# One layer-pair kernel for a graph and expert network on one core: gathered rows added by the DMA that gathers them, a multiplication moved to GpSimd, and other step lengths in the planner

## The chip, the cores and the metric

The kernel runs on one core of a Trainium2 chip. A core has five engines that each work through their own list of instructions in order: TensorE (PE; its weight loads are shown apart as PEld), VectorE (DVE), ScalarE (ACT), GpSimd (POOL) and SyncE (SP, which here only issues DMA transfers). Sixteen DMA engines move the data that any of them asks for. The metric is the device time of one launch in microseconds (us); lower is better.

## What is computed

Two layers over 2708 rows of 256 channels, in float32. Each layer has a graph attention over a 2708 x 2708 matrix and then a mixture of 8 experts of which every row uses 2; the first layer also has causal attention before its experts. Cut to what matters here:

```python
def _L0_gnn_ref(nodes, adj_bias_mat, weight, conv_weight1, conv_weight2, bias):
    h = nodes @ weight
    logits = h @ conv_weight1 + (h @ conv_weight2).T
    coefs = softmax(leaky_relu(logits, 0.2) + adj_bias_mat, axis=-1)
    return coefs @ h + bias

def _L0_ffn_ref(x, ...):                       # T = 2708, 4 heads, 2 key heads, head size 64
    h = _rmsnorm(x, ln1_w); q, k, v = h @ wq.T, h @ wk.T, h @ wv.T     # then rotary on q and k
    att = softmax(where(causal, q @ k.T / sqrt(64), -1e30))
    x = x + (att @ v) @ wo.T
    flat = _rmsnorm(x, ln2_w)
    # top 2 of 8 experts by softmax(flat @ router_w.T), weights normalised to sum 1
    out = sum(weights[:, e:e+1] * ((silu(flat @ w1[e].T) * (flat @ w3[e].T)) @ w2[e].T) for e in range(8))
    return x + out

x = x + _L0_gnn_ref(_layernorm(x), adj, ...)
x = x + _L0_ffn_ref(_layernorm(x)[None], ...)[0]
x = x + _L1_gnn_ref(_layernorm(x), adj, ...)   # masked by adj != 0 or the diagonal
x = x + _L1_ffn_ref(_layernorm(x)[None], ...)[0]
```

In the first layer the matrix holds values up to 1e9 that are added to the logits. So each row's softmax picks the one column with the largest value, and the graph attention of a row is the row of h at that column. The kernel uses this: it searches the largest value of each matrix row and its index, and gathers that row of h. (It counts whether the two largest values lie far enough apart, and would run a general version otherwise.)

## The kernel before

The rows are cut into 22 tiles of 128 (the last has 20). Four stages follow each other on the core: `first` (graph and causal attention of layer 0, its routing, and some blocks of its experts), `experts_blocks` for layer 0, `second` (graph attention of layer 1, its routing) and `experts_blocks` for layer 1. In the trace, the experts' first matmul (line 2015) of layer 0 begins at 526.7 us.

**The order of the work in `first` and `second`** comes from a planner, `Plan` (line 70). Each step is added with an engine, a planned length in us, the steps it needs, the buffers it takes and gives back, a rank, and for transfers a time `lands` until the data is there. `Plan.issue` then simulates the engines with these lengths and writes the instructions in the order in which the steps start, the lowest rank first among those that can start soon. Only the order comes from the lengths; on the chip each engine takes its list in this order and waits for semaphores where it must. Where the planner sees TensorE idle for 1 us or more, `fill` puts in matmuls that nobody uses (tile `nobody`, line 1259), to keep TensorE's clock up.

**What `first` does for each tile** (`tile_in`, line 956):

- `load`: SyncE loads 128 rows of the matrix (1354 KB) into one of three places of `arena`.
- `top` and `index` (lines 968 and 972): VectorE searches the largest values of each row and the index of the largest.
- `narrow` and `save`: ScalarE casts the matrix tile to bfloat16, SyncE stores it for layer 1.
- `fetch` (line 987): GpSimd issues an indirect DMA that gathers for each of the 128 rows the row of `hd` (h in DRAM, written by `project`) at the found index into a tile `xg`, 3 buffers.
- `stats` (line 995): VectorE adds `xg` to the tile of `X` (which lies in SBUF for the whole stage) and takes mean and variance of the sum. `power` and `norm`: GpSimd and ScalarE normalise it into `XB`.
- `turn`, `back`, `times`, `leave`: TensorE transposes the tile of `X`, multiplies it by the query, key and value weights, ScalarE moves the result.
- `both` (on GpSimd): the rotary step; `turn_qk` and `keep`: its transposition into `qT` and `kT`.

Before the tiles, `project` computes h for each pair of tiles; its step `bias` (line 904) adds the graph attention's bias to `X` on GpSimd. The list `biased` holds these steps; `stored` holds the writes of h.

**The causal attention** runs by pairs of tiles (`pair`, line 1074). For a pair that starts at tile t0: scores and their exponentials block by block, causal masks on GpSimd (`mask`, line 1104), the products with V on TensorE (`values`), and from the fourth pair on the sums of the exponentials on VectorE (`sums`, line 1131, tile `es`). Then:

- `leave`: ScalarE copies the products to `ob` in SBUF.
- `spread` (line 1167): TensorE brings the sums to all partitions, in a PSUM bank of the kind `mm` (2 banks).
- `weigh` (line 1176): VectorE takes the reciprocal of the sums into `yT` and multiplies `ob` by it. It gives back the `mm` bank and `ob`.
- `project_out`, `join`, `sum_up`, `store`: the output projection for each tile of the pair, its additions to `XB` and `X`, and the store.

GpSimd's list holds, besides the steps named, the scatters of routed rows to the experts' buffer (line 1803) and the accumulations of expert results in DRAM (`add_rows`, line 609). VectorE's list holds the searches, statistics, sums and routing, in one order.

In `second`, five loads bring `X` back from DRAM (line 1511); their steps have planned landing times.

Of the kernel before, what the change touches and what calls it, by code (L numbers as in the profile page):

```python
# [10 lines left out]
F32 = mybir.dt.float32  # L11
AF = mybir.ActivationFunctionType
ALU = mybir.AluOpType
AX = mybir.AxisListType
I32 = mybir.dt.int32
BF16 = mybir.dt.bfloat16
NEEDS = mybir.DependencyInfo(mybir.DependencyClass.Sync, mybir.DependencyReason.DATA)
PE, SP = mybir.EngineType.PE, mybir.EngineType.SP
PSUM = bass.MemoryType.PSUM

P = 128
N = 2708
C = 256
# [5 lines left out]
NREP = NH // NKV  # L29
# [14 lines left out]
LATE, LATE_T = ((7, 4), (7, 5)), 12  # L44
# [25 lines left out]
class Plan:  # L70
# [16 lines left out]
    def add(self, engine, length, run, needs=(), take=(), give=(), rank=0.0, lands=0.0):  # L87
        step = dict(engine=engine, length=length, run=run, needs=[n for n in needs if n is not None],
                    take=take, give=give, rank=rank, lands=lands, end=None)
        self.steps.append(step)  # L90
        return step
# [54 lines left out]
def adj_ffn_kernel(ctx, tc, x, adj, vecs, bias_rows, tab, w_gnn0, w_gnn1, wqkv, wo,  # L146
                   r0, r1, w1_0, w3_0, w2_0, w1_1, w3_1, w2_1, out):
    nc = tc.nc
# [633 lines left out]
    def first(X, XB, norms, tops, hd, mb, xs, acc, arena, load_weights):  # L782
# [11 lines left out]
        with ExitStack() as s:  # L794
            ap = s.enter_context(tc.tile_pool(name="attn", bufs=1))
            af = s.enter_context(tc.tile_pool(name="af", bufs=2))
            adjp = s.enter_context(tc.tile_pool(name="adjf", bufs=3))
            ab = s.enter_context(tc.tile_pool(name="ab", bufs=2))
# [20 lines left out]
            def tr_tile():  # L819
# [3 lines left out]
                        z=2, qk=2, es=1, ob=2, yT=2, mb=2, rT=1, adj0=1, adj1=1, adj2=1, low0=1, low1=1, low2=1)  # L823
            add = plan.add
# [3 lines left out]
            for a, b in ((0, 4), (4, NT - 1)):  # L828
                loads.append(add("SP", 0.5, lambda a=a, b=b: nc.sync.dma_start(
                    out=X[:, a:b, :], in_=x[a * P:b * P, :].rearrange("(t p) c -> p t c", p=P)),  # L830
                    rank=-9.0, lands=1.5 + 0.4 * (b - a)))
            loads.append(add("SP", 0.5, lambda: nc.sync.dma_start(
                out=X[:rows(NT - 1), NT - 1, :], in_=x[(NT - 1) * P:N, :]), rank=-9.0, lands=9.0))
# [20 lines left out]
            a = add("SP", 1.2, load_wq, loads, take=["e"], rank=1.5, lands=3.0)  # L854
# [22 lines left out]
            centred = centre(wgc, wg[0], C, [wg_in], -3.0), centre(wq_sb, wq_sb, 2 * C, [wq_in], -0.5)  # L877

            stored, biased = [], []
# [76 lines left out]
            def tile_in(t):  # L956
                r = rows(t)
                v = {}
                rank = float(t)
# [24 lines left out]
                def save(h):  # L984
                    nc.sync.dma_start(out=mb[t * P:(t + 1) * P, h * HALF:(h + 1) * HALF], in_=v["m", h])

                def fetch():
                    v["xg"] = af.tile([P, C], F32, tag="xg", name="xg", bufs=3)
                    nc.gpsimd.indirect_dma_start(
                        out=v["xg"][:r], out_offset=None, in_=hd[:, :],  # L990
                        in_offset=bass.IndirectOffsetOnAxis(ap=v["ix"][:r, 0:1].bitcast(I32), axis=0))

                xt = X[:r, t, :]

                def stats():
                    nc.vector.tensor_tensor(xt, xt, v["xg"][:r], ALU.add)
                    v["mv"] = moments(xt, r)
                    v["pv"] = small.tile([P, 2], F32, tag="pv2", name="pv2")
                    nc.vector.scalar_tensor_tensor(v["pv"][:r], two_eps[:r, 0, :], v["mv"][:r, 1:2], two_eps[:r, 1, :],
                                                   ALU.mult, ALU.add)  # L1000
# [45 lines left out]
                def keep():  # L1046
# [3 lines left out]
                a = loaded[t] = add("SP", 5.8, load, take=[f"adj{t % 3}", f"low{t % 3}", "tb"], rank=rank,  # L1050
                                    lands=1.5)
                a = add("DVE", 2.97, top, [a], rank=rank + 2)
                b = a
                for h in range(2):

                    b = add("ACT", 1.4, lambda h=h: narrow(h), [b, stored[-1]], take=["mb"], give=[f"low{t % 3}"] * h, rank=rank + 4)
                    add("SP", 0.4, lambda h=h: save(h), [b], give=["mb"], rank=rank, lands=3.0)
                a = add("DVE", 3.05, index, [a], take=["ix"], give=[f"adj{t % 3}"], rank=rank + 2)
                a = add("POOL", 1.1, fetch, [a] + stored, take=["xg"], give=["ix"], rank=rank, lands=2.2)
                a = add("DVE", 1.4, stats, [a, biased[t]], take=["mv"], give=["xg"], rank=rank)  # L1060
                c = add("POOL", 1.2, power, [a], give=["mv"], rank=rank)
                b = add("ACT", 0.6, norm, [c], rank=rank)
                a = add("PE", 0.5, turn, [a], take=["mm"], rank=rank)
                a = add("ACT", 0.4, back, [a], take=["hT"], give=["mm"], rank=rank)
                a = add("PE", 2.0, times, [a, centred[1]], take=["mm"], give=["hT"], rank=rank)
                c = add("ACT", 0.8, leave, [a, c], take=["z"], give=["mm"], rank=rank)
                a = add("POOL", 3.4, both, [c], take=["qk"], give=["tb"], rank=rank)
                add("ACT", 0.7, lengths, [c, a], give=["z"], rank=rank + 6)
                a = add("PE", 0.65, turn_qk, [a], take=["mm"], give=["qk"], rank=rank)
                a = add("ACT", 0.7, keep, [a], give=["mm"], rank=rank)  # L1070
                made[t] = a, b

# [1 line left out]
            def pair(t0):  # L1074
# [3 lines left out]
                v = {}  # L1078
                on_pe = t0 < PE_SUMS
                rank = t0 + 2.5  # L1080
                ready = [made[t0][0], made[t0 + 1][0]]
                end = None
# [4 lines left out]
                for n in range(0, t0 + 2, 2):  # L1087
# [54 lines left out]
                    es = []  # L1142
                    for sb in two:
                        a = add("PE", 1.0, lambda f=scores, sb=sb: f(sb), ready, take=["st"], rank=rank)
# [4 lines left out]
                        es.append(b)  # L1149
                    last = n == t0  # L1150
                    if on_pe:
                        end = add("PE", 3.0, values, es + [end], take=["o", "zs"] if n == 0 else [],
                                  give=["e"] * 2, rank=rank)
                        ends = [end]
                    else:
                        end = add("PE", 2.0, values, es + [end], take=["o"] if n == 0 else [], rank=rank)
                        ends = [add("DVE", 2.4 if n else 1.2, sums, es + [ends[0] if n else None, end],
                                    take=["es"] if n == 0 else [], give=["e"] * 2, rank=rank)]

                def leave():  # L1160
# [6 lines left out]
                def spread():  # L1167
# [3 lines left out]
                    else:  # L1171
                        for g in range(NKV):
                            nc.tensor.matmul(v["z"][g * HD:(g + 1) * HD, :], allones[:, :HD], v["es"][:, g, :],
                                             start=True, stop=True)

                def weigh():
                    v["yT"] = ab.tile([P, 2, NREP, P], F32, tag="yT", name="yT")
                    y = v["yT"].rearrange("p t j c -> p (t j c)")
                    nc.vector.reciprocal(y, v["z"])
                    nc.vector.tensor_tensor(y, v["ob"], y, ALU.mult)  # L1180

                a = add("ACT", 1.2 if on_pe else 0.6, leave, [end], take=["ob", "es"] if on_pe else ["ob"],
                        give=["o", "zs"] if on_pe else ["o"], rank=rank - 1)
                a = add("PE", 1.0, spread, [a] + ends, take=["mm"], give=["es"], rank=rank - 1)
                a = add("DVE", 4.2, weigh, [a], take=["yT"], give=["mm", "ob"], rank=rank - 1)
                for i in range(2):
                    t = t0 + i
                    r = rows(t)

                    def project_out(i=i, t=t, r=r):  # L1190
                        v["pw", i] = pw = mm_tile()
                        for j in range(NREP):
                            nc.tensor.matmul(pw[:r, :C], v["yT"][:, i, j, :r], wo_sb[:, j, :],
                                             start=(j == 0), stop=(j == NREP - 1))

                    def join(i=i, t=t, r=r):
                        nc.vector.tensor_tensor(XB[:r, t, :], v["pw", i][:r, :C], XB[:r, t, :], ALU.add)

                    def sum_up(t=t, r=r):
                        nc.gpsimd.tensor_tensor(out=X[:r, t, :], in0=X[:r, t, :], in1=XB[:r, t, :], op=ALU.add)  # L1200

                    def store(t=t, r=r):
                        nc.sync.dma_start(out=acc[t * P:t * P + r, :], in_=X[:r, t, :])

                    b = add("PE", 1.0, project_out, [a], take=["mm"], give=["yT"] if i else [], rank=rank - 1)
                    b = add("DVE", 0.45, join, [b, made[t][1]], give=["mm"], rank=rank - 1)
                    joined.append(b)
                    b = add("POOL", 1.1, sum_up, [b], rank=rank + 3)
                    summed.append(b)
                    add("SP", 0.4, store, [b], rank=rank + 3)  # L1210
# [197 lines left out]
    def second(X, XB, xs0, x1, x2, sd, mb, xs, arena, load_weights):  # L1408
# [9 lines left out]
        with ExitStack() as s:  # L1418
# [93 lines left out]
            for a, b in zip((0,) + ends, ends):  # L1512
                loads.append(add("SP", 0.45 * (b - a), lambda a=a, b=b: nc.sync.dma_start(
                    out=X[:, a:b, :], in_=x1[a * P:b * P, :].rearrange("(t p) c -> p t c", p=P)),
                    late, rank=-9.0, lands=2.0 if 0 < a < LATE_T else 7.0))
                if b == LATE_T:
                    late = some_blocks(add, 0, [(*b, []) for b in LATE], [XR[:, k, :] for k in range(len(LATE))], [],
                                       lambda e: weights_at(arena[:, WE:]), xs0, x1, new, named, -20.0)
                    for e in late:
                        e["needs"] += loads  # L1520
# [697 lines left out]
```

## Time and profile before

| what | us |
|---|---|
| median of 3 runs (lowest, highest) | 1566.0 (1564.26, 1569.35) |
| the profiled execution, its own time | 1573.58 |
| its span, from the first to the last instruction | 1571.9 |
| `first`, 0 to 527 us of the span: PE, DVE, ACT, POOL busy | 466.4, 397.8, 296.6, 270.6 |
| experts of layer 0, 527 to 867 us: PE busy | 339.8 of 340 |
| `second`, 867 to 1216 us: PE, DVE busy | 333.0, 209.0 of 349 |
| experts of layer 1, 1216 to 1572 us: PE busy | 340.4 of 356 |
| granted TensorE clock, mean | 0.969 |

All views below are of this one profiled execution. In a line of a group of instructions stand line, engine, operation, output and inputs with their shapes, the count, then the busy us in total and the mean in ns of one, then the idle time of the engine just before them and what ended it. In a line of the waits stand who waited, for whom, us in total, how often and, where it is given, the longest. In a line of a stretch stand its bounds and length, and per engine the busy us and the count of instructions. TensorE instructions are recorded twice for each float32 matmul, so counts of records are twice those of matmuls.

### The profile page before, as it was taken

The numbers are of one execution on the slowest core, as the hardware profiler recorded it, in microseconds if no ns is written. First come the engines' busy times: TensorE is split into PE (matmuls) and PEld (weight loads), VectorE is DVE, ScalarE is ACT, GpSimd is POOL, SyncE is SP. The second block draws the span as 40 slices with busy tenths as digits, with TensorE's granted clock in tenths as the row PEclk, the third lists the DMA queues.
The fourth block names the chain that finished last, engine by engine and source line by source line (L and its number), as shares of the span: only waits on it lengthen the run. The fifth ranks groups of instructions, "written<-read, shape, count | busy, mean of one in ns | idle before, by whom it ended". The sixth has DMA issues, their size and how long they took to land. (4 is left out here: it accounts for less than half of the span.)

```text
span 1571.9 us, 23225 instructions
## 1 busy us (share of the span) xinstructions
PE 1479.6 (94%) x8926; PEld 1154.0 (73%) x8926; DVE 747.2 (48%) x1483; ACT 552.5 (35%) x1068; POOL 500.9 (32%) x684
## 2 busy tenths in 40 slices
PE   6888899989999999999999799999999999999996
PEld 5633333323335999999999778888768999999995
DVE  5798899876576222222221464857754222222221
ACT  3676567555544111111221353443332111111110
POOL 5654468483152222222112210030434122222221
PEclk9989899999999999999999899999999999999998
DMA  7688654650012323333221670632414233332211
GB/s 261 225 286 298 209 194 176 198 171 7 8 49 80 88 53 88 90 91 89 35 38 22 152 150 1 131 89 82 146 53 112 78 83 87 74 76 62 33 33 17
DMA packets 165998, 165.68 MB, mean 105 GB/s; under 512 B 81378, under 2 KB 145550, under 8 KB 163168
## 3 DMA queue, kind: packets, MB, share of 16 engines
q1 hardware_dynamic: 142582, 134.26, 28.0%
q0 software_dynamic: 19024, 26.24, 9.2%
q10 hardware_dynamic: 4270, 3.58, 0.7%
q8 instruction: 72, 1.18, 0.3%
q14 instruction: 50, 0.41, 0.1%
HBM read 87.38 MB, written 61.55 MB: 95 GB/s over the span
## 5 line engine op out<-in xcount | busy, mean ns | idle before, releaser
L2015 PEld LDWEIGHTS pup<-xTs,arena 128*128 128x128 f32 x2772 | 317.8, 190 | 3.7 <-ACT xTs L283 0.7
L2015 PE MATMUL pup<-xTs,arena 128*128 128x128 f32 x2772 | 319.7, 275 | 0.5 <-ACT xTs L283 0.5
L2020 DVE TENSOR_TENSOR hT<-sl,pup 128x640 f32<-128x640 f32 x87 | 71.4, 821 | 448.0 <-ACT sl L2019 448.0
L2019 ACT ACTIVATE sl<-pup 128x640 f32<-128x640 f32 x87 | 61.3, 704 | 503.3 <-PE pup L2015 499.2
L1576 PE MATMUL po<-hb,PT 128*128 128x257 f32 (+2 forms) x968 | 226.0, 388 | 3.6 <-DVE PT L1569 3.6
L1576 PEld LDWEIGHTS po<-hb,PT 128*128 128x128 f32 (+2 forms) x968 | 176.1, 188 | 42.6 <-issue 11.9
L2029 PE MATMUL y<-arena,hT 128*128 128x256 f32 x756 | 173.8, 380 | 0.6 <-DVE ys L2031 0.6
L1101 ACT ACTIVATE e<-stt 128x1024 f32<-128x1024 f32 (+1 forms) x132 | 125.9, 985 | 93.6 <-PE stt L1095 69.2
L2029 PEld LDWEIGHTS y<-arena,hT 128*128 128x128 f32 x756 | 138.7, 190 | 17.3 <-DVE ys L2031 1.0
L1140 DVE TENSOR_TENSOR es<-es,e 128x1024 f32<-128x1024 f32 x104 | 130.6, 1256 | 31.2 <-ACT e L1101 24.5
L611 POOL DMA_INDIRECT out<-ys,xt x44 | 68.4, 1554 | 231.1 <-DVE ys L2031 221.9
L1095 PE MATMUL stt<-qT,kT 64*128 64x512 f32 (+1 forms) x528 | 133.4, 612 | 6.7 <-ACT e L1101 6.7
L1803 POOL DMA_INDIRECT xs<-XR,place x88 | 95.2, 1081 | 135.0 <-DVE mk L1563 40.7
L611 POOL DMA_INDIRECT acc<-ys,xt x43 | 66.9, 1555 | 222.6 <-DVE ys L2031 221.1
L1121 PE MATMUL o<-e,V 128*64 128x512 f32 (+1 forms) x528 | 129.7, 614 | 1.2 <-ACT e L1101 1.2
L2015 PE MATMUL pup<-xTs,room 128*128 128x128 f32 (+1 forms) x1056 | 123.8, 275 | 0.0
L2015 PEld LDWEIGHTS pup<-xTs,room 128*128 128x128 f32 (+1 forms) x1056 | 121.9, 190 | 1.2
L1554 ACT ACTIVATE E<-sb,dcol 128x768 f32<-128x768 f32 (+1 forms) x88 | 75.2, 859 | 105.0 <-DVE PT L1569 102.1
L1095 PEld LDWEIGHTS stt<-qT,kT 64*128 64x128 f32 x528 | 44.0, 187 | 80.2 <-issue 62.9
L1121 PEld LDWEIGHTS o<-e,V 128*64 128x64 f32 x528 | 34.1, 141 | 73.0 <-issue 54.3
L2031 DVE TENSOR_SCALAR ys<-y,xt 128x256 f32<-128x256 f32 x87 | 42.0, 483 | 53.9 <-PE y L2029 53.9
L2029 PE MATMUL y<-room,hT 128*128 128x256 f32 x288 | 66.1, 379 | 0.0
(276 smaller groups left out, 1885.6 us busy)
## 6 DMA issues: line engine op xcount, KB each, us to landing
arena<-in_adj SPq DMA_DIRECT2D x21, 1354.0 KB
arena<-in_w SPq DMA_DIRECT2D x36, 640.0 KB
mb<-mb SPq DMA_DIRECT2D x44, 352.0 KB
xs<-none SPq DMA_DIRECT2D x16, 804.0 KB
xt<-xs SPq DMA_DIRECT2D x87, 134.0 KB
room<-in_w SPq DMA_DIRECT2D x12, 640.0 KB
acc<-X SPq DMA_DIRECT2D x21, 128.0 KB
out<-X SPq DMA_DIRECT2D x21, 128.0 KB
```

The lines of the kernel that those rows point to most:

```text
L611: nc.gpsimd.indirect_dma_start(out=acc[:, :], out_offset=bass.IndirectOffsetOnAxis(ap=xt[:, C:C + 1].bitcast(I32), axis=0), in_=ys, in_off ...
L1095: nc.tensor.matmul(st[:r, g, c0(sb):], kT[a:b, sb * P:sb * P + r], qT[a:b, t0 + (sb == t0 + 1):t0 + 2, :, :], start=True, stop=True)
L1101: nc.scalar.activation(e[:r, :, c0(sb):], v[sb, "st"][:r, :, c0(sb):], AF.Exp, scale=1.0 / HD ** 0.5)
L1121: nc.tensor.matmul(v["o"][g * HD:(g + 1) * HD, c:], V[:r, sb, g * HD:(g + 1) * HD], v[sb][:r, g, c:], start=(n + i == 0), stop=(n + i == t ...
L1140: nc.vector.tensor_tensor(es, es, v[sb][:r, :, c:], ALU.add)
L1554: nc.scalar.activation(e[:q, :n], sb[:q, i0:i1], AF.Exp, bias=dcol[:q, j:j + 1], scale=SLOPE - 1.0)
L1576: nc.tensor.matmul(v["po", i][:r, :F], v["PT", j][:q, a:a + r], hb[:q, j, :], start=(j == 0), stop=(j == NT - 1))
L1803: i = nc.gpsimd.indirect_dma_start(out=xs[:, :], out_offset=bass.IndirectOffsetOnAxis(ap=at, axis=0), in_=src, in_offset=None)
L2015: nc.tensor.matmul(pp[:to, n, :], wn[:, c, :], xT[:, c, :], start=(c == 0), stop=(c == KC - 1))
L2019: nc.scalar.activation(sl, pp[:, :NF, :], AF.Silu)
L2020: nc.vector.tensor_tensor(hT[:, :NF, :], sl, pp[:, NF:2 * NF, :], ALU.mult)
L2029: nc.tensor.matmul(y, hT[:, n, :], w[3][:, n, :], start=(n == 0), stop=(n == NHC - 1))
```

## The change

Three edits, all in `first` but for one number in `second`:

1. `fetch` gathers straight into the tile of `X` and has the DMA add to what stands there (`compute_op=ALU.add`). The tile `xg` and the addition in `stats` go. `fetch` now needs the tile's `bias` step. (`xg` stays as the name of the buffers of some experts' results.)
2. `weigh` is cut in two: the reciprocal stays on VectorE (`turn_over`, gives back the `mm` bank), and the multiplication by it goes to GpSimd (`weigh`, gives back `ob`).
3. Planned lengths: several of TensorE's and VectorE's steps, and the landing time of the first load of `X` in `second`.

```diff
+                xt = X[:r, t, :]
+
                 def fetch():
-                    v["xg"] = af.tile([P, C], F32, tag="xg", name="xg", bufs=3)
                     nc.gpsimd.indirect_dma_start(
-                        out=v["xg"][:r], out_offset=None, in_=hd[:, :],
-                        in_offset=bass.IndirectOffsetOnAxis(ap=v["ix"][:r, 0:1].bitcast(I32), axis=0))
-
-                xt = X[:r, t, :]
+                        out=xt, out_offset=None, in_=hd[:, :],
+                        in_offset=bass.IndirectOffsetOnAxis(ap=v["ix"][:r, 0:1].bitcast(I32), axis=0),
+                        compute_op=ALU.add)
 
                 def stats():
-                    nc.vector.tensor_tensor(xt, xt, v["xg"][:r], ALU.add)
                     v["mv"] = moments(xt, r)
...
-                a = add("POOL", 1.1, fetch, [a] + stored, take=["xg"], give=["ix"], rank=rank, lands=2.2)
-                a = add("DVE", 1.4, stats, [a, biased[t]], take=["mv"], give=["xg"], rank=rank)
+                a = add("POOL", 1.6, fetch, [a, biased[t]] + stored, give=["ix"], rank=rank, lands=2.5)
+                a = add("DVE", 0.95, stats, [a], take=["mv"], rank=rank)
...
-                a = add("PE", 0.5, turn, [a], take=["mm"], rank=rank)
+                a = add("PE", 0.25, turn, [a], take=["mm"], rank=rank)
...
-                a = add("PE", 2.0, times, [a, centred[1]], take=["mm"], give=["hT"], rank=rank)
+                a = add("PE", 1.75, times, [a, centred[1]], take=["mm"], give=["hT"], rank=rank)
...
-                a = add("PE", 0.65, turn_qk, [a], take=["mm"], give=["qk"], rank=rank)
+                a = add("PE", 0.35, turn_qk, [a], take=["mm"], give=["qk"], rank=rank)
...
-                        end = add("PE", 3.0, values, es + [end], take=["o", "zs"] if n == 0 else [],
+                        end = add("PE", 2.9, values, es + [end], take=["o", "zs"] if n == 0 else [],
...
-                        end = add("PE", 2.0, values, es + [end], take=["o"] if n == 0 else [], rank=rank)
-                        ends = [add("DVE", 2.4 if n else 1.2, sums, es + [ends[0] if n else None, end],
+                        end = add("PE", 1.9, values, es + [end], take=["o"] if n == 0 else [], rank=rank)
+                        ends = [add("DVE", 2.46 if n else 1.25, sums, es + [ends[0] if n else None, end],
...
+                def turn_over():
+                    v["yT"] = ab.tile([P, 2, NREP, P], F32, tag="yT", name="yT")
+                    nc.vector.reciprocal(v["yT"].rearrange("p t j c -> p (t j c)"), v["z"])
+
                 def weigh():
-                    v["yT"] = ab.tile([P, 2, NREP, P], F32, tag="yT", name="yT")
                     y = v["yT"].rearrange("p t j c -> p (t j c)")
-                    nc.vector.reciprocal(y, v["z"])
-                    nc.vector.tensor_tensor(y, v["ob"], y, ALU.mult)
+                    nc.gpsimd.tensor_tensor(out=y, in0=v["ob"], in1=y, op=ALU.mult)
...
-                a = add("PE", 1.0, spread, [a] + ends, take=["mm"], give=["es"], rank=rank - 1)
-                a = add("DVE", 4.2, weigh, [a], take=["yT"], give=["mm", "ob"], rank=rank - 1)
+                a = add("PE", 0.9, spread, [a] + ends, take=["mm"], give=["es"], rank=rank - 1)
+                a = add("DVE", 3.4, turn_over, [a], take=["yT"], give=["mm"], rank=rank - 1)
+                a = add("POOL", 1.6, weigh, [a], give=["ob"], rank=rank - 1)
...
-                    b = add("PE", 1.0, project_out, [a], take=["mm"], give=["yT"] if i else [], rank=rank - 1)
+                    b = add("PE", 0.9, project_out, [a], take=["mm"], give=["yT"] if i else [], rank=rank - 1)
...
-                    late, rank=-9.0, lands=2.0 if 0 < a < LATE_T else 7.0))
+                    late, rank=-9.0, lands=2.0 if 0 < a < LATE_T else 14.0 if a == 0 else 7.0))
```

## The prediction

> **What bounds the kernel now.** I read the table of stages first: the change touches the first stage (0 to 527 us of the span), and in the third only one planned landing time. The chain of waits shows only the last 5 us here, so I took the busy times of all engines in the two halves of the first stage, then the slices of the page, then who waited for whom.
>
> ```profile
> core 0: us, PE busy (x) PEld busy (x) DVE busy (x) ACT busy (x) POOL busy (x), PEclk, DMA share, GB/s
> 60.00:340.00 280.00, 243.36 (x993) 100.84 (x993) 245.55 (x277) 183.59 (x323) 171.60 (x250) 0.92 0.65 223
> 340.00:527.00 187.00, 177.54 (x860) 82.51 (x861) 112.68 (x169) 89.26 (x148) 64.68 (x97) 0.98 0.18 58
> ```
>
> From 60 to 340 us VectorE is busy 245.6 of 280 us, and TensorE 243.4: TensorE idles 36.6 us there and only 9.5 us in the 187 us after it. The max and index searches over the adjacency rows (22 of each, 2.97 us a piece) end at 326.8 us; until then VectorE's in-order list sets the pace, after it TensorE does. The waits of the first stage (who waited for whom, us in total, times, longest) say what the idle time of both was:
>
> ```profile
> DVE X L996 <- DMA xg<-hd,ix: 19.8, 9, 3.6
> ...
> PE pm L1044 <- POOL qk L1038: 11.9, 9, 3.3
> PE stt L1095 <- ACT e L1101: 6.7, 6, 3.3
> PE pm L1173 <- DVE es L1140: 5.9, 3, 2.9
> PE pm L1193 <- DVE yT L1180: 4.6, 6, 1.1
> ```
>
> VectorE's largest wait is for the gathered rows (19.8 us). TensorE's waits are short and spread: each is for a step that follows VectorE's list.
>
> The pieces that the change moves:
>
> ```profile
> L996 DVE TENSOR_TENSOR X<-X,xg 128x256 f32<-128x256 f32 (+1 forms) x22 | 10.8, 490 | 19.9 <-DMA xg<-hd,ix 19.8
> L1180 DVE TENSOR_TENSOR yT<-osb,yT 128x512 f32<-128x512 f32 x11 | 8.6, 784 | 1.1
> L989 POOL DMA_INDIRECT xg<-hd,ix x22 | 24.9, 1131 | 29.0 <-DVE ix L972 20.4 <-issue 8.3 <-ACT mb L982 0.2
> L611 POOL DMA_INDIRECT acc<-ys,xt x43: 1550/1551/1569, 540.8 to 862.4; - x43
> ```
>
> **What the Trainium skill says.** "DMA: Bandwidth & Descriptors", section SWDGE vs HWDGE vs iDMA: an accumulating DMA can only be issued from GpSimd, and each DMA engine takes turns between its queues packet by packet. The trace has both kinds of transfer; the queue's line for one gather of 128 rows, and for one accumulation of 128 rows (7 us windows both):
>
> ```profile
> q0 software_dynamic: 48, 0.13, 6.3%
> ...
> q0 software_dynamic: 144, 0.13, 16.1%
> ```
>
> Same bytes, three times the packets, and 1.13 instead of 0.44 us of each DMA engine. The same page, section Rules for kernel authors: an accumulating DMA must wait for earlier writers of its bytes; so the gather must now follow the bias add of its tile of x. "SBUF — State Buffer", section Who interferes with whom: a VectorE instruction with two SBUF inputs and a GpSimd instruction that reads SBUF exclude each other. The trace agrees: the rotary add L1038 takes 0.99 us alone and 1.86 us at 320.9 us beside two sums L1140, which then take 3.38 instead of 2.5 us. "GPSIMD Engine Reference", section Performance versus the Vector engine: two-input arithmetic is about twice as slow there; here 128x256 takes 0.73 us and 128x384 1.00 us on GpSimd, so I estimate 1.27 us for 128x512, against 0.69 us on VectorE.
>
> **The change part by part** (the built order of both kernels is known, their times not).
>
> *Adds leave VectorE.* 22 adds by 0.490 us: -10.8 us, all before 340 us. TensorE's transposition of x can then start without the add, too.
>
> *Multiplications leave VectorE.* 11 by 0.784 = 8.6 us, of which 7 (5.5 us) start before 340 us, where VectorE counts. The four later ones are hidden behind TensorE already, and I cost them at nothing.
>
> *The gather becomes an accumulation.* On GpSimd's queue 1.55 instead of 1.13 us, 22 by 0.42 = +9.2 us; 11 multiplications add 14 us. GpSimd's busy time from 60 to 340 us goes from 172 to about 190 of 280 us: room, but everything there is in order. What counts is the landing. Where VectorE waited, the gathered rows had landed 6.4 to 8.6 us after the gather began on GpSimd under load (118.37 to 126.94, 77.36 to 84.70), and 2.5 us in the quiet (331.61 to 334.10). The new one takes +0.4 us to issue, +0.7 us of transfer, and, for six more turns of each engine beside the adjacency loads, an unknown rest. Bounds: below by nothing (a part may overlap); above by about 5 us, if each extra packet waits like a gather's own under load. Nearest evidence: the accumulation at 503.62, beside weight loads (DMA 0.9 busy), had all its packets done by about 508.6, 5 us after its start. I take +1.5 us in all.
>
> What that costs follows from the slack, the VectorE work that stands between an index search and the statistics that need its rows. Counting instructions of the built orders by their measured lengths, the slack before is under 8 us for 13 of 22 tiles. Stalls summed as (landing minus slack): 17 us at a landing of 7 us, 28 at 8; the measured 19.8 fits 7.3 us. After, fewer tiles are short (8 under 8 us): 15 us at 8, 25 at 9, 35 at 10, 49 at 11, 63 at 12. At 7.3 + 1.5 = 8.8 us: 23 us, +3 against before.
>
> *The multiplication waits on GpSimd.* It waits for the reciprocal; behind it in GpSimd's order stand mostly the causal masks (L1110 before), for which TensorE's products wait. And in 5 of 11 pairs VectorE's next instruction after the reciprocal is a sum of two SBUF tiles (1.22 us), which excludes the multiplication. Bounds 0 and 11 by 1.3 = 14 us; mostly GpSimd is the one that is held, so I take 1.5 us on VectorE in its critical part. The output projection gets its input about 0.8 us later than now; other TensorE work stands beside it, and without that cover it would be 11 by 0.8 = 9 us.
>
> *Lengths.* They change the order only. The planner now thinks TensorE shorter, sees more gaps and puts in 31 more idle matmuls in this stage (110 instead of 79). At 0.327 us each 10 us, if the gaps weren't there; TensorE does idle 36.6 us in the part where nearly all of them stand, so nothing is charged. By the order, the last index search comes after 252 instead of 282 us of VectorE work: tiles are prepared sooner, sums later. In the third stage the landing of the first x tiles (planned 7, now 14 us) swaps some statistics before 911 us, where the first product waited for the mask's DMA anyway: 0, within 2 us either way.
>
> *Sum.* VectorE's part to the last index: -10.8 - 5.5 + 3 + 1.5 = -11.8 us. TensorE must fill the time: its idle there would fall from 36.6 to 25 us, but part of it hangs on GpSimd's rotary work (11.9 us), which gets later. I pass on two thirds: -8 us. The profiled execution took 1573.58 us, span 1571.9, so 1565.6 for it; it lies 7.6 us above the median of the runs, 1566.0, from which I forecast **1558 us**.
>
> **The rivals.**
> *A, as above:* 1546 to 1561 us. For it: VectorE busy 88% where TensorE idles, and TensorE at 95% right after. Chance 0.55.
> *B, the relief is absorbed:* TensorE takes no more than now, since its own clock (granted 0.92 in this part), the masks and rotary work on the fuller GpSimd, and the additional idle matmuls hold it. Then the 11.8 us become VectorE idle: about 1565 us, 1561 to 1571. For it: 11.9 us of TensorE's waits are for GpSimd already; against: GpSimd has 90 us of room. Chance 0.24.
> *C, slower:* the accumulating gather lands too late, at the statistics of each tile, with the next max and index search in order behind them. It decides from a landing of about 10 us, 3 us later than the gather's: there the stalls, 36 us less the 20 of now, have eaten the 16.3 us of adds and multiplications that leave. At 12 us they are 63, 43 more than now, so VectorE's list is 27 us longer; half to two thirds of that reach the end: about 1582 us. At 11 us it is about 1573. For it: three times the packets in turn-taking with loads that keep the DMA engines 65% busy; against: the loaded accumulation at 503.62. Chance 0.21.
>
> **How the numbers follow.** About 0.3%, 4.7 us, is what this measurement can tell from no change. Faster (below 1561.3): A and a little of B, 0.57. Same: most of B and the mildest of C, 0.22. Slower (over 1570.7): 0.21. A's own range is 1546 to 1561. The range reaches up through B into C as far as a landing of 11 to 12 us, and down to all of VectorE's gain with fewer stalls: 1543 to 1577.
>
> **What would show it.** Right: no VectorE add after the gather; VectorE's last index search ends near 312 us instead of 326.8; its waits for the gathered x stay near 20 us; TensorE's idle from 60 to 340 us falls under 30 us; the experts' first matmul comes near 519 instead of 526.7 us, and the later stages keep their lengths. Wrong: waits of VectorE's statistics for the gather above 40 us (C); the first stage as long as before with a longer idle VectorE, and TensorE waiting for GpSimd's masks or rotary add (B); the multiplication on GpSimd at 2.5 us or more; the sums L1140 longer than 1.26 us on average; or a third stage that changes by more than 2 us.

## Result and profile after

Four runs each on the same chip: before 1565.13 us (1563.68 to 1569.35), after **1553.43 us** (1550.42 to 1555.93). The ratio is 0.992, 95% interval 0.9894 to 0.9947: 12.5 us less by the ratio, forecast 8. Run once more beside the last experiments, the kernel after gave 0.9877 (0.9858 to 0.9897). The profiled execution took 1553.19 us, its span is 1551.5.

In the profiled executions 17.2 of the 20.4 us lie in the first stage: the experts' first matmul starts at 509.5 us instead of 526.7. The table of stages of the kernel after, for the two stretches that the prediction shows of before:

```profile
core 0: us, PE busy (x) PEld busy (x) DVE busy (x) ACT busy (x) POOL busy (x), PEclk, DMA share, GB/s
60.00:340.00 280.00, 247.55 (x1085) 105.94 (x1084) 247.02 (x254) 192.02 (x342) 208.03 (x275) 0.97 0.73 237
340.00:527.00 187.00, 180.63 (x957) 94.58 (x956) 108.04 (x166) 84.69 (x139) 60.72 (x85) 0.99 0.13 40
```

TensorE idles 32.5 instead of 36.6 us from 60 to 340, 4.1 us less, where the prediction looked for 8 and for less than 30. What stands out is PEclk, TensorE's mean granted clock as a share of full speed: 0.97 instead of 0.92. VectorE is as busy there as before (247.0 beside 245.6 us), though 16.3 us of its work were to leave: its list was reordered too. Its last index search ends at 296.1 us, before at 326.8; the prediction expected about 312. The groups of the kernel after that answer to those of before:

```profile
L1139 DVE TENSOR_TENSOR es<-es,e 128x1024 f32<-128x1024 f32 x104 | 138.0, 1327 | 29.4 <-ACT e L1100 22.9
...
L990 POOL DMA_INDIRECT X<-hd,ix x22 | 37.2, 1692 | 18.1 <-issue 9.3 <-DVE ix L972 8.7 <-POOL mb L981 0.2
...
L1261 PE MATMUL nobody<-before,allones 128*128 128x128 f32 x220 | 35.0, 318 | 9.5 <-DVE before L225 9.5
...
L1181 POOL TENSOR_TENSOR yT<-osb,yT 128x512 f32<-128x512 f32 x11 | 17.1, 1552 | 16.6 <-DVE yT L1177 16.3 <-DVE rm L431 0.3
```

The add is gone; the gather takes GpSimd 1.69 us (before 1.13) and the multiplication 1.55; the sums grew from 1256 to 1327 ns; the idle matmuls (two records each) take 35.0 us (before 25.9). The waits of this kernel from 0 to 527 us, first VectorE's, then TensorE's:

```profile
DVE st L261 <- DMA X<-hd,ix: 18.8, 11, 5.8
...
PE pm L1043 <- POOL qk L1037: 6.9, 5, 3.2
PE pm L1020 <- ACT hTt L1015: 5.0, 4, 2.4
PE pm L1195 <- POOL yT L1181: 4.5, 5, 1.8
PE stt L1094 <- ACT e L1100: 4.5, 7, 1.5
PE pm L1011 <- DMA X<-hd,ix: 4.5, 4, 1.5
```

VectorE waits for the gathered rows as long as before (18.8 beside 19.8 us). TensorE's waits for the rotary add, for the exponentials and for VectorE's sums (0.8 us in all, before 5.9) are shorter; those for X (4.5 us, before 2.4) and for the transposed rows hT (5.0, before 0.6) are longer.

**Where the time went, read from TensorE.** The windows of the kernel before around its longest stretch of low clock, and TensorE's timeline there (in brackets what it idled for):

```profile
178.00:182.00 4.00, 1.11 (x4) 0.23 (x4) 3.86 (x5) 1.09 (x2) 2.53 (x3) 0.95 0.03 8
182.00:186.00 4.00, 4.00 (x16) 2.56 (x16) 4.00 (x2) 2.33 (x4) 0.00 (x0) 0.50 0.00 0
186.00:190.00 4.00, 4.00 (x13) 2.21 (x10) 2.06 (x5) 1.11 (x1) 0.00 (x0) 0.50 0.78 267
190.00:194.00 4.00, 4.00 (x7) 2.01 (x6) 3.00 (x16) 0.84 (x2) 0.27 (x1) 0.50 0.69 260
```

```profile
176.84 1.13 PE L1095 MATMUL stt<-qT,kT 64*128 64x512 f32 x4
180.89 1.29 PE L1173 MATMUL pm<-es,allones 128*64 128x512 f32 x4 [2.93 <-DVE es L1140]
182.12 1.88 PE L417 MATMUL pg<-rwn,rT 128*128 128x8 f32 x8
183.93 3.68 PE L1121 MATMUL o<-e,V 128*64 128x512 f32 x8
```

TensorE waits 2.93 us for the sums; right after, its clock is at half for 13.65 us, and the eight L1121 records take 3.68 us where eight took 1.94 just before, at 173.05. If the whole stretch is put down to that gap, it cost 2.93 us and then up to 6.8 more. The trace's record of the granted clock has only full and half in this stage, in pieces of 3.41 us and multiples. The Trainium skill, "TensorE: Matmul & The Clock Gate", Part 1, says the same: two states, half and full, decided over windows of 3413 ns by how busy TensorE was. The trace agrees on the two states and on the length of the pieces. The page puts a half clock down to about 3.4 us without work and its end to about 3.4 us of work; the trace confirms neither, for here 2.93 us without work were enough, and TensorE shows no idle time in these 13.65 us. What sets the length of such a stretch stays open.

From this a sum can be made for each trace, from 30 us to the experts' first matmul: half of the time in which TensorE did useful work at half clock; its idle time; the busy time of the idle matmuls; and a rest. The stretch that is summed, before and then after:

```profile
core 0: us, PE busy (x) PEld busy (x) DVE busy (x) ACT busy (x) POOL busy (x), PEclk, DMA share, GB/s
30.00:526.70 496.70, 448.73 (x1985) 206.87 (x1985) 382.92 (x494) 290.60 (x506) 255.84 (x376) 0.94 0.46 156
```

```profile
30.00:509.50 479.50, 438.98 (x2046) 207.33 (x2046) 375.57 (x459) 290.10 (x506) 287.49 (x387) 0.97 0.49 160
```

| kernel | experts' first matmul | lost to half clock | idle gaps | idle matmuls | rest | ratio of the runs |
|---|---|---|---|---|---|---|
| before | 526.7 | 26.6 | 48.0 | 19.5 | 402.6 | 1 |
| after | 509.5 | 9.8 | 40.5 | 28.7 | 400.5 | 0.992 |
| e1 | 522.3 | 18.4 | 52.6 | 19.2 | 402.1 | 0.9982 |
| e2 | 519.9 | 15.1 | 46.5 | 25.3 | 403.0 | 0.9966 |
| e3 | 516.4 | 12.5 | 46.1 | 27.0 | 400.8 | 0.9925 |
| e6 | 532.6 | 26.1 | 51.7 | 23.5 | 401.3 | 1.0037 |
| e7 | 503.4 | 14.2 | 58.5 | 0 | 400.7 | 0.9859 |
| e8 | 524.1 | 16.4 | 48.7 | 25.8 | 403.2 | 1.002 |
| e9 | 520.5 | 20.5 | 48.2 | 20.7 | 401.1 | 0.9946 |
| e10 | 518.8 | 16.9 | 43.7 | 28.3 | 399.9 | 0.9943 |
| e11 (after) | 506.6 | 7.6 | 40.9 | 26.9 | 401.2 | 0.9877 |
| e12 | 519.4 | 26.0 | 62.7 | 0 | 400.7 | 0.9962 |
| e13 | 507.3 | 14.2 | 48.4 | 11.0 | 403.7 | 0.985 |
| e14 | 506.8 | 8.2 | 38.9 | 28.7 | 401.0 | 0.989 |

The rest is TensorE's useful work at full clock: 399.9 to 403.7 us in all fourteen. So what differs between the kernels is the other three columns. Before to after: half clock -16.8, idle -7.5, idle matmuls +9.2, rest -2.1, together -17.2 us. This is bookkeeping: it says where TensorE's time went, not who made the gaps; that takes the experiments. Each row is one execution; the profiled one of before took 8 us more than the median of its series, so its 26.6 may be high.

The mean granted clock is on record for every run of the experiments, over the whole program. (1 - clock) times the span, averaged over the runs and compared with the kernel before on the same chip, says the same for the main pairs: 12.1 us less in e3, of 12.0 us gained in mean time; 8.3 of 8.5 in e10; 17.7 of 20.3 in e11. It does not say it everywhere: e2 has 12.9 us less for 5.9 gained, e7 4.2 for 21.8. This count includes half clock in which TensorE had nothing to do or ran idle matmuls.

### The profile page after: what moved, and what is told of

Its sections match the earlier page's. It is cut to its first block, busy times and chain, and to the rows that moved or that the text cites. A ratio compares the mean times of both kernels' runs of the same rounds, so it can differ in the third digit from the quotient of the medians.

```text
span 1551.5 us, 23359 instructions
## 1 busy us (share of the span) xinstructions
PE 1468.3 (95%) x8988; PEld 1153.4 (74%) x8988; DVE 740.9 (48%) x1450; ACT 551.9 (36%) x1068; POOL 533.0 (34%) x695
## 5 line engine op out<-in xcount | busy, mean ns | idle before, releaser
L1139 DVE TENSOR_TENSOR es<-es,e 128x1024 f32<-128x1024 f32 x104 | 138.0, 1327 | 29.4 <-ACT e L1100 22.9
L2031 PEld LDWEIGHTS y<-arena,hT 128*128 128x128 f32 x756 | 138.8, 190 | 17.2 <-DVE ys L2033 1.0
L1120 PE MATMUL o<-e,V 128*64 128x512 f32 (+1 forms) x528 | 122.4, 586 | 0.0
L1120 PEld LDWEIGHTS o<-e,V 128*64 128x64 f32 x528 | 32.9, 136 | 68.6 <-issue 52.6
```

The source lines that it names most:

```text
L1120: nc.tensor.matmul(v["o"][g * HD:(g + 1) * HD, c:], V[:r, sb, g * HD:(g + 1) * HD], v[sb][:r, g, c:], start=(n + i == 0), stop=(n + i == t ...
L1139: nc.vector.tensor_tensor(es, es, v[sb][:r, :, c:], ALU.add)
L2031: nc.tensor.matmul(y, hT[:, n, :], w[3][:, n, :], start=(n == 0), stop=(n == NHC - 1))
```

## The experiments

My theory was the prediction's: VectorE's shorter list gives the gain. Its rivals were that the new planned lengths give it, by their order or by their 31 more idle matmuls, and that the accumulating gather or the fuller GpSimd takes back what VectorE gives. All ratios are to the kernel before on the same chip.

**One part at a time.** The kernel before with one part of the diff, and the kernel after without the lengths.

e1: `fetch` accumulates into X, the add is gone, with the lengths of these two steps.

> The kernel before with the accumulating gather alone (its own two planned lengths with it); multiplications stay on VectorE, all other planned lengths are the old ones. If the gain comes from VectorE's shorter list: 22 adds of 0.49 us leave it, so the first stage is shorter by 5 to 9 us and the whole by as much: 1556 to 1560 us beside 1565. If the gain of the whole change comes from the planned lengths: within 2 us of the kernel before. If the gather's landing (7 to 9 us under load) costs what the adds give back: 1565 or above, with waits of the statistics for X above 30 us.

Measured: 0.9982 (0.9971 to 0.9993), -2.8 us: less than a shorter VectorE list was to give, though the last index search starts 33 us earlier than before.

e2: the multiplication on GpSimd, with its own step.

> The kernel before with the 11 multiplications moved to GpSimd alone. If VectorE's list is what counts: 5.5 us leave its part before the last index search, less what the sums beside the multiplication lose (the sums L1140 took 1.33 instead of 1.26 us each in the changed kernel, 7 us over 104 of them), so between 4 us faster and 2 us slower. If the fuller GpSimd delays masks and projection: 3 to 8 us slower, with waits of the projection for yT above 10 us. If the multiplication carries the gain: 5 us faster or more.

Measured: 0.9966 (0.9954 to 0.9978), -5.4 us. But this also reorders: 110 idle matmuls, and the last index search 37 us earlier.

e3: only the numbers, here two of the ten.

```
-                a = add("PE", 0.5, turn, [a], take=["mm"], rank=rank)
+                a = add("PE", 0.25, turn, [a], take=["mm"], rank=rank)
...
-                a = add("PE", 1.0, spread, [a] + ends, take=["mm"], give=["es"], rank=rank - 1)
+                a = add("PE", 0.9, spread, [a] + ends, take=["mm"], give=["es"], rank=rank - 1)
...
```

> The kernel before with the new planned lengths alone (TensorE's steps, the sums, and 14 us for the first x tiles of the third stage): the order changes and 115 instead of 79 idle matmuls stand in the first stage, the work of each engine stays. If the gain comes from VectorE's shorter list: within 3 us of the kernel before. If order and idle matmuls (a TensorE clock of 0.97 instead of 0.92 between 60 and 340 us) carry it: 6 to 12 us faster with a granted clock of 0.96 or more there.

Measured: 0.9925 (0.9912 to 0.9938), -11.8 us: about what the whole change gave in its first series, with all of VectorE's work in place.

e6: the reverse.

> The kernel after with the old planned lengths of TensorE's steps, the sums and the third stage; gather and multiplication changed. If VectorE's shorter list is the cause: 9 to 12 us faster than the kernel before, as the kernel after (11.7). If the lengths carry it: under 4 us faster.

Measured: 1.0037 (1.0024 to 1.005), +5.8 us; a kernel slower than before was in neither expectation. The first half of the stage in e3 and then in e6, from the table of stages:

```profile
60.00:340.00 280.00, 244.63 (x1073) 104.86 (x1071) 252.00 (x279) 187.57 (x328) 179.88 (x254) 0.95 0.64 221
```

```profile
60.00:340.00 280.00, 238.50 (x982) 99.71 (x980) 232.68 (x257) 183.73 (x318) 189.72 (x252) 0.91 0.72 233
```

VectorE is busy 19 us less in e6 than in e3 in this stretch, and e6 is 17.6 us slower. Its last index search starts at 298.1 us; in e3 at 330.4, later than before (323.8). So neither VectorE's busy time nor the end of its searches sets the time. The clock does go with it: 0.91 against 0.95. My theory in its simple form falls here.

**Order or idle matmuls?** A gap that the list sees is filled with idle matmuls without moving any other step, so the two can be separated.

e7: after without them.

```
-            plan.fillers = [("zs", 1, idle("zs", afp)), ("o", 1, idle("o", afp))]
+            plan.fillers = []
```

> The kernel after without the 110 idle matmuls of the first stage; the order of all other work is the same. In the runs so far the first stage follows the TensorE clock granted from 60 to 340 us (before 0.92 and 526.7 us, new lengths alone 0.95 and 516.4, after 0.97 and 509.5). If the idle matmuls hold the clock up: the clock falls to 0.92 or less there and the gain is gone, ratio 1.000 or above. If they only fill time that the order leaves: ratio stays 0.990 to 0.994, clock 0.96 or more.

Measured: 0.9859 (0.9844 to 0.9875), -22.1 us. Neither expectation held: the idle matmuls don't carry the gain, and taken out they don't cost it. In the table against after: idle matmuls -28.7, idle gaps +18.0, half clock +4.4. They bought clock, for more than it was worth.

e8: the filling made denser (the share of a gap that is filled, 0.75 before) in the order of before. e9 makes it thinner, 0.51, in the order of the new lengths.

```
+            plan.FILL = 1.05
```

> The kernel before, its order unchanged, with 114 instead of 79 idle matmuls in the first stage (the same gaps of the list filled more densely). If the number of idle matmuls carries what the new lengths brought (12 us): 6 to 12 us faster, ratio 0.992 to 0.996. If the new order carries it: within 2 us, ratio 0.9985 to 1.0015.

> The kernel before with the new planned lengths alone, its idle matmuls thinned from 115 to 77 (before: 79), the order of all other work as with the new lengths. If the order carries the 12 us: ratio 0.991 to 0.995, as with 115. If the number of idle matmuls carries it: ratio 0.998 to 1.002.

Measured: e8 1.002 (1.0006 to 1.0034), e9 0.9946 (0.9932 to 0.996). The order brings 8.5 us of e3's 11.8 with as few idle matmuls as before; their number brings nothing in the old order. e3 and e9 themselves are not told apart (their intervals overlap).

e12: the kernel before without its 79.

> The kernel before without its 79 idle matmuls of the first stage, order unchanged. Taken out of the kernel after, they gave about 9 us. If idle matmuls cost their own time wherever they stand: 5 to 9 us faster, ratio 0.994 to 0.997. If they earn in the old order, with its longer gaps of TensorE, what they cost: ratio 0.998 to 1.003, with more half clock than the 61 us of before.

Measured: 0.9962 (0.9949 to 0.9975), -6.0 us. Of 19.5 us that they took, idle gaps took over 14.7, and the useful work lost no more to half clock than before (26.0 beside 26.6). By the granted clock of all runs there is 7.9 us more half clock without them, and yet the kernel is faster.

**VectorE's work at a fixed order.** The order of after is kept, and the work is put back.

```
                 def stats():
+                    nc.vector.tensor_tensor(xt, xt, xt, ALU.max)
                     v["mv"] = moments(xt, r)
...
-                    nc.gpsimd.tensor_tensor(out=y, in0=v["ob"], in1=y, op=ALU.mult)
+                    nc.vector.tensor_tensor(y, v["ob"], y, ALU.mult)
```

e10: both lines.

> The kernel after, its order unchanged, with VectorE's work put back: the multiplications run on VectorE at the same place of the list, and ahead of each tile's statistics stands an operation of the size of the add that was taken out (the maximum of x with itself, which leaves x as it is). If VectorE's shorter list carries the gain, as the prediction said: 16 us of VectorE work are back before 300 us, two thirds of it reach the end, so the ratio is 0.998 to 1.002. If order and TensorE's clock carry it: ratio 0.991 to 0.995, with VectorE's waits shorter instead.

e14: the second alone, with the kernel after (e11) on the same chip.

> The kernel after once more, as the yardstick of this series: ratio 0.990 to 0.9945 (0.992 measured before), TensorE idle for 2 us or more about 6 times between 30 us and the experts' first matmul, and about 27 us of half clock there.

> The kernel after, its order unchanged, with the 11 multiplications on VectorE at the same place of the list (0.78 instead of 1.55 us each); the accumulating gather stays. If moving them is worth what the prediction said (5.5 us less on VectorE, 1.5 us given back, two thirds passed on): ratio 2 us above the yardstick of this series (0.0015 to 0.003). If the sums beside them[...] (1327 instead of 1256 ns) and the later projection cost more than that: the same ratio or one below it, with the sums back at 1.26 us. With both parts put back on VectorE the ratio was 0.9943; what is above this run there belongs to the adds.

Measured: e10 0.9943 (0.9929 to 0.9956), e11 0.9877 (0.9858 to 0.9897), e14 0.989 (0.9868 to 0.9912). e11 itself is below its expected range: the kernel after gained 19.4 us in this series and 12.5 in the first, and the two intervals barely touch, so a comparison across series can be off by that much. e14 is 2 us above e11, inside both intervals: what moving the multiplications is worth is not told from nothing. e10 lies in the range that was expected if order and clock carry the gain. But it ran on another chip than e11; its interval lies above e11's and overlaps that of after's first series (0.9894 to 0.9947). So VectorE's work, put back in the order of after, costs between 3.6 and 10.4 us by the middle values, and the prediction's 8 us lie inside: here a shorter VectorE list does count, as it did not in the old order (e6). e10 and e14 differ in the adds alone. Their first stages differ by 12.0 us (518.8 and 506.8), 8.7 of them in half clock and 4.8 in idle gaps, and the waits of e10 show how an add can cost TensorE more than VectorE:

```profile
DVE X L996 <- DMA X<-hd,ix: 17.2, 10, 5.6
...
PE pm L1012 <- DVE X L996: 9.4, 4, 3.7
```

The transposition of x stands behind the add, which stands behind the landing. In after it waits for the landing alone (4.5 us, 2.4 in e11). That is one order's case: in the kernel before, this wait for the add was 2.4 us.

**Only the long gaps filled.** e13 is after with idle matmuls only where the list sees 2 us or more.

```
+            plan.GAP_MIN = 2.0
```

> The kernel after with idle matmuls only in gaps that the list thinks 2.0 us or longer (50 instead of 110; before: 1.0 us). In every trace so far a half clock of 3.4 us or a multiple follows a gap of TensorE of about 2 us or more, and hardly ever a shorter one. If idle matmuls in short gaps only cost and those in long ones keep the clock up: ratio 0.984 to 0.987, as without any or better. If they help nowhere, the time lies between: 0.988 to 0.990. If short gaps need them: 0.992 or above.

Measured: 0.985 (0.9833 to 0.9867), -23.6 us. That is as fast as e7, in the range that was expected if filling short gaps only costs. Against e11 beside it, 1553.23 and 1555.1 us, the intervals still overlap (0.9858 to 0.9867), and in its profile less filling (-15.9) is balanced by idle (+7.5) and half clock (+6.6). e7 and e13 beat the kernel before clearly; that they also beat the kernel after, by 2 to 11 us, is likely and not shown.

Left untried: the accumulating gather alone at a fixed order with the old landing, and e7 with the gather of before.

## Why the prediction was right in size and wrong in its sum

- *What bounds.* "VectorE's in-order list sets the pace" until the last index search: wrong as it stands. e3 and e6 order the other way, and in e1 and e2 the searches end at 293.5 and 289.6 us, over 30 us early, for a gain of 2.8 and 5.4. VectorE matters where it makes a gap in TensorE's work, and that depends on the order: in the order of after, its work put back costs 3.6 to 10.4 us (e10).
- *Adds leave.* All 22 are gone, the operation put back in e10 took 0.503 us each. That x can be transposed without the add was said, and had no price; e10 shows 9.4 us of TensorE waiting there, the kernel before only 2.4.
- *Multiplications leave.* 5.5 us were counted, less 1.5; at a fixed order 2 us, not told from nothing (e14). The duration on GpSimd was estimated well for the undisturbed case (1.27 us, median 1271 ns), but the mean is 1552 ns, and GpSimd is busy 208.0 us from 60 to 340, where about 190 were estimated. The sums, which were the sign of wrong, grew by 71 ns, 7.4 us in all, instead of 1.5; but with the multiplications back on VectorE they still took 1303 ns (e14), and 1252 in e6, which has them on GpSimd. So most of it goes with the order; that the order of after puts more of GpSimd's work beside them is likely and was not counted.
- *The gather.* On GpSimd 1.69 us, estimated 1.55. In the 17 gathers before the first scatter of rows the last packet came a median 6.7 us after the gather's start, before 5.7: 1.0 us later, with 1.5 counted. The stalls that were to grow from 20 to 23 us stayed at 18.8 (16.6 in e11; 26.4 in the order of e6). Rival C, which needed over 36 us of them, did not happen in any order tried.
- *Lengths.* "They change the order only" and "nothing is charged" is the step that failed, twice over. The order alone is worth 8.5 to 11.8 us (e9, e3). And the idle matmuls took 9.2 us more, in gaps that were partly not there: removing all of them from before opened gaps of only 14.7 us for 19.5.
- *The sum.* TensorE's idle was to fall by 8 us; it fell by 4.1 from 60 to 340 us and by 7.5 in the whole stage, and the added idle matmuls took that back. The gain itself is TensorE's half clock, 26.6 to 9.8 us, which the sum didn't have: the prediction named the granted clock of 0.92 only as something that would hold TensorE back (rival B), not as something that a gap causes. The number came out by luck, because terms of opposite sign were missing, and only in the first series: in that of e11 the gain is 19.4 us, more than twice the 8.
- *Third stage.* From its first product to the second experts' first matmul 302.0 us before, 298.6 after, more than the 2 us allowed. But this stretch differs by more than that between traces with the same planned landing: it took 299.3 to 307.7 us in the six with the old 7 us, 298.2 to 305.3 in the eight with the new 14 us. What the landing is worth is not told.

The parts don't add: -2.8, -5.4 and -11.8 alone, +5.8 for the first two together, -12 to -19 for all. Each edit reorders the whole stage, and in the old order the gaps and the clock that come of it weighed more than the instructions that left.

## What to carry to other kernels

Where a planner orders the work, test its numbers alone and the new instructions in a fixed order; the change as written shows neither. Sum TensorE's useful work, its gaps, its half clock and its filling for the stage before asking which engine is busiest: here that sum closed to within 4 us over fourteen traces, and VectorE's busy time did not even order them. Count gaps of 2 us and longer twice, for themselves and for the clock, and take fillers out once before trusting them.

## What the runs showed of the hardware

In the first stages of the fourteen traces (from 30 us to the experts' first matmul), 85 of 112 TensorE gaps of 2 us or more had a half clock beginning near their end (from 2.5 us before to 3.6 us after it), against 54 of 201 gaps of 0.8 to 2 us; an instant taken at random has one as near in 10% of all cases. Seen from the other side, 81 of the 114 half clocks that begin there lie near a gap of 2 us or more, and 113 near one of at least 0.8 us. So shorter gaps are followed by a half clock too, if less often, and more often than e13's expectation ("hardly ever") had it. Each half clock lasted 3.41 us or a multiple, up to 13.65 us; with TensorE at work throughout, that costs 1.7 to 6.8 us on top of the gap. The Trainium skill, "TensorE: Matmul & The Clock Gate", section HAM oscillation, warns of gaps longer than about 3.4 us; here 68 of the 85 were shorter. That the gap is the cause is the reading of these traces: no run changed a single gap by itself. Taking out all idle matmuls, which opened gaps, went with more half clock both times: by the granted clock of all runs 7.9 us more in e12 than in before, and 10.3 more in e7 than in e11, there on two chips.
